# Four score banks in one tile, token preparation in three steps, and cosine norms taken apart in a four-layer transformer kernel

## The chip, the cores and the metric

The kernel runs on one core of a Trainium2 chip, in one launch. The metric is the device time of that launch in microseconds (us), the median over several runs. The core has a matrix engine (TensorE, PE in the profile, with its weight loads shown apart as PEld), VectorE (DVE), ScalarE (ACT), GpSimd (POOL) and SyncE (SP), from whose queue this kernel issues all of its DMA transfers. Matrix products land in PSUM, which this program uses as eight banks of 128 x 512 fp32. All arithmetic is fp32.

## The reference, cut to what matters

Input `x` has 8 batches of 256 tokens and 512 features. Four layers follow each other:

```python
# layer 0: RMS norm, 8 query heads of width 64 on one key/value head, rotary, softmax; then a gated MLP
h = ada_rms(x);  q, k, v = rope(h @ Wq.T), rope(h @ Wk.T), h @ Wv.T
x = x + softmax(q @ k.T / 8) @ v @ Wo.T
x = x + (silu(h2 @ Wg.T) * (h2 @ Wu.T)) @ Wd.T

# layer 1: LayerNorm with a condition, 16 heads of width 32, cosine attention; then a GELU MLP
qn = q / max(norm(q), 1e-12) * sm          # per token and head, over 32 numbers
kn = k / max(norm(k), 1e-12)
x = x + (softmax(qn @ kn.T + bias) @ v @ Wproj.T + bproj) * gamma1
x = x + (gelu(h2 @ Wfc1.T + bfc1) @ Wfc2.T + bfc2) * gamma2

# layer 2: 16 query heads of width 32, 4 key/value heads, rotary, a sparse mask
x = x + softmax(where(mask, -inf, q @ k.T / sqrt(32))) @ v @ Wo.T

# layer 3: eight experts 64 -> 256 -> 64 on slices of the features, LayerNorm, silu, projection
x = x + silu(layernorm(experts(x)) * (1 + scale) + shift) @ out_W + out_b
```

## The kernel before, in words

The residual `x` stays in SBUF as 16 tiles of 128 tokens. A batch is two such tiles. The stages run one after another: attention 0, MLP 0, attention 1, MLP 1, attention 2, experts.

**Order.** The program is traced in Python and a planner then orders the instructions of each engine: it may run an instruction earlier than the trace order has it, as soon as its inputs and its buffer are free, and it puts the semaphore waits in. A tile belongs to a tag; a tag has as many buffers as `BUFS` says, and a new tile of a tag waits until the users of the tile before it in its buffer are done.

**PSUM.** Two tags share the eight banks. Tag `C` has four buffers of one bank: projections, transposes, weighted sums. Tag `A` has four buffers of one bank as well: the scores of the four heads of a group (`scored`, L645), the four accumulators of the MLP's second product (`lower`, L955), and the hidden values of the experts (L1621).

**Attention** (`attend`). The loop runs over batches `b` and groups `g` of four heads: two groups in a batch in layer 0, four in layers 1 and 2. One turn traces the scores of this group (`scored`), transposes of two heads of the group before (`turned`, L702, with copies out of PSUM on L460 and L464), the softmax of this group (`softmax`: L667 or L659 on DVE, exponentials L672 on ACT, reciprocals of the sums sent through DRAM by the SP queue, L685 and L690), then slices of queued work (`some`: the projection of the next batch, the output product of the batch before), the other two transposes, the weighted sum (`weighted`, L717) and its division (`divided`, L732). The probability tiles, tag `p`, have seven buffers.

**Preparation** (`prepare`, `normed`, `fetch`, `h`). Two batches ahead, after the softmax of group 0, the tokens of a batch are normalised for their projection: statistics (L431, L432), the power -1/2 on POOL (L440), the two normalisations (L450), a DVE transposition in 32 x 32 blocks (L515), four DMAs to DRAM (L520). `fetch` brings them back, feature-major, in eight DMAs (L539), or in one for an MLP (L533). `h` scales and shifts them (L472, L474). The target tag `hT` has two buffers.

**Cosine norms** (`project1`, layer 1). For each of the two token tiles of a batch, the product of the queries goes to SBUF with its bias (L1367) and is squared (L1369) and summed by heads (L1370); the keys are copied (L1373), squared out of SBUF (L1375) and summed (L1376). POOL then takes the maximum with 1e-24 (L1378) and the power -1/2 (L1379) of all 32 sums in one instruction each, multiplies the query half by `sm` (L1380), and multiplies queries and keys by their norms (L1383). Their transposes are L1355.

**MLP** (`mlp`). Both products use a Strassen scheme of seven products. `lower` accumulates in four banks over four steps `p`; after the fourth, `combined` reads them (L966 on ACT, L968 to L973 on DVE), and the next `lower` with `p == 0` takes four banks anew.

Of the kernel before, what the change touches and what calls it, by code (L numbers as in the profile page):

```python
# [28 lines left out]
AF = mybir.ActivationFunctionType  # L29
ALU = mybir.AluOpType  # L30
# [3 lines left out]
P = 128  # L34
# [5 lines left out]

BUFS = {
    "n": 4, "hT": 2, "qT": 2, "kT": 2, "v": 2, "ctxT": 6, "p": 7, "qk": 4, "row": 3, "wbig": 8,
    "A": 4, "C": 4,
}
MASKED = -1.0e30

# [125 lines left out]
class Program:  # L172
# [21 lines left out]

    def bank(self, tag):
        return self.t([P, 512], tag)

# [219 lines left out]

    def normed(self, xs, eps, rms=False, outs=None):


        nc = self.nc
        n = len(xs)
        mv = self.t([P, n, 2], f"mv{n}", 2)
        r = self.t([P, n], f"r{n}", 2)
        for i, x in enumerate(xs):
            st = self.t([P, 6], "st", 3)  # L430
            nc.vector.bn_stats(st, x)  # L431
            nc.vector.bn_aggr(mv[:, i, :], st)  # L432
        mean, var = mv[:, :, 0], mv[:, :, 1]
        if rms:
            nc.vector.tensor_tensor(r, mean, mean, ALU.mult)
            nc.vector.tensor_tensor(r, r, var, ALU.add)
            nc.gpsimd.tensor_scalar(r, r, eps, None, ALU.add)
        else:
            nc.gpsimd.tensor_scalar(r, var, eps, None, ALU.add)  # L439
        nc.gpsimd.tensor_tensor(r, r, self.neg_half[:, 0:n], ALU.pow)  # L440
        rows = []
        for i, x in enumerate(xs):
            if outs is None:
                y = self.bank("n")
            else:
                y, x = outs[i], x.rearrange("p (k c i) -> p c k i", k=KC, c=4)
            if rms:
                nc.vector.tensor_scalar(y, x, r[:, i : i + 1], None, ALU.mult)
            else:
                nc.vector.tensor_scalar(  # L450
                    y, x, mv[:, i, 0:1], r[:, i : i + 1], ALU.subtract, ALU.mult
                )
            rows.append(y)
        return rows
# [47 lines left out]
    def prepare(self, name, b, quick=False):  # L502

        eps, _, _, _, rms, blocks = self.stage(name)
        xs = [self.x[TB * b + t] for t in range(TB)]
        hT = self.t([P, KC * S], "hT")
        if quick:
            self.ready[name, b] = [hT, self.normed(xs, eps, rms), None, 0]  # L510
            return
        nc = self.nc
        y = hT.rearrange("p (c k t i) -> p c k t i", c=4, k=KC, t=TB)
        self.normed(xs, eps, rms, [y[:, :, :, t, :] for t in range(TB)])
        nc.vector.transpose(hT, hT)  # L515
        kept = self.turns[self.n_turn % 3]
        self.n_turn += 1
        to = kept.rearrange("(c i) (a x) -> a i c x", c=4, a=4)
        for a in range(4):
            nc.sync.dma_start(  # L520
                to[a], hT[32 * a : 32 * a + 32, :].rearrange("p (c x) -> p c x", c=4)
            )
        self.ready[name, b] = [hT, None, kept, 0]

    def fetch(self, calls):

# [14 lines left out]
    def h(self, name, b, quick=False):  # L541


        if (name, b) not in self.ready:
            self.prepare(name, b, quick)
            yield None
            self.fetch(1)
        hT, rows, _, at = self.ready[name, b]
        while self.calls < at:
            yield None  # L550
        self.ready.pop((name, b))
        _, mod, scale_at, shift_at, _, blocks = self.stage(name)
        if blocks:
            place = hT.rearrange("p (a k q) -> p k a q", a=4, k=KC)
        else:
            place = hT.rearrange("p (k t) -> p k t", k=KC)

        def placed(i, c, in_):
            scale = mod[:, scale_at + c, b : b + 1]
            shift = None if shift_at is None else mod[:, shift_at + c, b : b + 1]  # L560
            self.modulated(i, place[:, c], in_, scale, shift)

        if rows is None:
            for c in range(KC):
                placed(c, c, place[:, c])
        else:

            def evacuate(c0, m):
                for c in range(2):
                    placed(c0 // 2, c0 + c, m[:, c, :])  # L570

            yield from self.feature_major(rows, evacuate)
        if blocks:
            return hT
        hT = place
        return hT
# [32 lines left out]
    def attend(self, name, n_groups, hd, project, value, finish, work, key_tiles=(2, 2), biased=None,  # L609
# [26 lines left out]

        def scored(b, g):
            lhs_rhs = [got[b][0](g, j) for j in range(4)]
            s = [self.bank("A") for _ in range(4)]
            rows = P // hd  # L640
            for j0 in range(0, 4, rows):
                for q in range(TB):
                    for j in range(j0, j0 + rows):
                        lhsT, rhs = lhs_rhs[j]
                        nc.tensor.matmul(  # L645
                            s[j][:, at[q] : at[q] + wide[q]], lhsT(q), rhs(wide[q]),
                            start=True, stop=True,
                        )
            return s
# [86 lines left out]
            chunks = ctx.pop(b)  # L736
            return finish(b, lambda k, t: chunks[k][:, t * P : (t + 1) * P])

        last = None
        for i in range(B * n_groups + 1):  # L740
            ahead = None
            if i < B * n_groups:
# [18 lines left out]
            if ahead is not None:  # L761
                ahead = (b, g, softmax(ahead[2]))
                if g == 0 and ahead_of:
                    for c in (1, 2) if b == 0 else (b + 2,):
                        if c < B:
                            self.prepare(name, c, quick=c == 1)
                        elif c == B and after is not None:
                            self.prepare(after, 0)
                elif g == 0 and b == B - 1:
                    self.prepare(after, 0)  # L770
            if last is None:
                self.some(3 * quantum)
            elif ahead is None and then is not None:
# [118 lines left out]
    def mlp(self, ups, downs, down_sums, load_ups, load_down, act, h, finish, tail):  # L892
# [52 lines left out]
        def lower(s, a, sums_of_a):  # L945
            hh, b, p = where(s)
            (y11, t3, y21, y22), (t1, t2, t4) = downs[4 * hh + p][:2]
            if p == 0:
                acc[:] = [self.bank("A") for _ in range(4)]
            s1, s2, s4 = [sums_of_a[:, i, :] for i in range(3)]  # L950
            for at, half, left, right in (
                (0, 0, a[:, 0, :], y11), (0, 1, a[:, 2, :], y21), (3, 0, a[:, 1, :], t3),
                (2, 0, s1, t1), (2, 1, s2, t2), (1, 0, s4, y22), (1, 1, a[:, 3, :], t4),
            ):
                nc.tensor.matmul(  # L955
                    acc[at][:, half * S : (half + 1) * S], left, right,
                    start=(p == 0 and half == 0), stop=(p == 3), skip_group_check=True,
                )
            if p == 3:
                combined(hh, b)  # L960
# [373 lines left out]
    def project1(self, b, got):  # L1334
# [8 lines left out]
        def part(t, i):  # L1343
            m = self.bank("C")
            yield from self.product_steps(
                m,
                lambda k: hT[:, k, t * P : (t + 1) * P],
                lambda k: w[:, k, i * D : (i + 1) * D],
            )
            return m  # L1350
# [11 lines left out]
        ready = []  # L1362
        for t in range(TB):
            ss = self.t([P, 32], "ss", 2)
            q = yield from part(t, 0)
            qs = self.bank("qk")
            nc.vector.tensor_tensor(qs, q, self.q_bias, ALU.add)  # L1367
            sq = self.bank("n")
            nc.scalar.activation(sq, qs, AF.Square)  # L1369
            nc.vector.tensor_reduce(ss[:, 0:16], heads(sq), AX.X, ALU.add)  # L1370
            k_ = yield from part(t, 1)
            ks = self.bank("qk")
            nc.scalar.copy(ks, k_)  # L1373
            sq = self.bank("n")
            nc.scalar.activation(sq, ks, AF.Square)  # L1375
            nc.vector.tensor_reduce(ss[:, 16:32], heads(sq), AX.X, ALU.add)  # L1376

            nc.gpsimd.tensor_scalar(ss, ss, 1e-24, None, ALU.max)  # L1378
            nc.gpsimd.tensor_tensor(ss, ss, self.neg_half, ALU.pow)  # L1379
            nc.gpsimd.tensor_tensor(ss[:, 0:16], ss[:, 0:16], self.sm, ALU.mult)  # L1380
            for y, at in ((qs, 0), (ks, 16)):
                by = ss[:, at : at + 16].unsqueeze(2).to_broadcast([P, 16, 32])
                nc.gpsimd.tensor_tensor(heads(y), heads(y), by, ALU.mult)  # L1383
            ready.append((qs, ks))
        qT = self.t([P, KC, S], "qT")
        kT = self.t([P, KC, S], "kT")
        v = self.t([P, TB, D], "v")
# [216 lines left out]
    def layer3(self):  # L1604
        nc = self.nc
        n_tiles = 4
        b1, b2 = self.v("b1"), self.v("b2")

        def two(tag):
# [4 lines left out]
        def hidden(xT, k):  # L1614

            got = [[], []]
            for f in range(2):
                ms = [self.bank("A") for _ in range(2)]
                for j in range(2):
                    rows = slice(64 * j, 64 * j + 64)  # L1620
                    nc.tensor.matmul(  # L1621
# [130 lines left out]
```

## Time and profile before

| | us |
|---|---|
| median of three runs | 2130.87 (2130.27 to 2134.04) |
| the profiled execution's own time | 2125.73 |
| its span | 2123.8 |
| PE busy in it | 2060.5 (97%) |
| DVE busy | 1349.5 (64%) |
| ACT busy | 761.1 (36%) |
| POOL busy | 291.3 (14%) |

The profile is of one execution. Its span is the time from the first to the last instruction; busy time is the time in which an engine executes. "PE C L702 <- DVE p L460" says that PE waited, before an instruction of line 702 that writes a tile of tag `C`, for DVE's instruction of line 460 that wrote a `p`. An fp32 product appears as two records. Stages by the trace: attention 0 until about 304 us, MLP 0 until about 905, attention 1 until about 1296, MLP 1 until about 1700, attention 2 until about 1968, experts until the end.

### The profile page before, as it was taken

The page shows a single profiled execution, that of the slowest core. Times are in us where ns is not written, and L with a number is a line of the kernel's source. Part 1 is how long each engine was busy: PE and PEld are TensorE (multiplying, and loading weights), DVE is VectorE, ACT ScalarE, POOL GpSimd, SP SyncE. Part 2 cuts the span into 40 slices and gives each one's busy share as a digit, 9 for nine tenths or more (in the row PEclk, how much of TensorE's full clock was granted, in tenths as well). Part 3 has the DMA queues.
Part 4 walks back from the last instruction along what each step waited for, and adds up shares of the span by engine and source line. Part 5 has one row for each costly group of instructions (what it writes and reads, how often), then busy time and mean ns, then how long its engine had stood idle before and what let it go on. Part 6 is the DMA issues. An engine that isn't in the chain of part 4 may idle for free.

```text
span 2123.8 us, 36492 instructions
## 1 busy us (share of the span) xinstructions
PE 2060.5 (97%) x13282; PEld 1523.8 (72%) x13282; DVE 1349.5 (64%) x4474; ACT 761.1 (36%) x2330; POOL 291.3 (14%) x308
## 2 busy tenths in 40 slices
PE   7999899999999999999999999999999989999999
PEld 4555569999999999855555547999999855555444
DVE  6856665656676555756666665776666777776333
ACT  3424321111111111245555663222222256566644
POOL 1101100000000000144444432000000101010220
PEclk9999999999999999999999999999999999999999
DMA  8320241211230100411112132233211222210001
GB/s 308 115 59 17 91 149 38 73 41 58 76 94 19 36 19 18 100 46 40 37 40 52 44 95 78 85 102 115 94 49 46 76 47 45 57 39 19 11 35 40
DMA packets 172147, 138.18 MB, mean 65 GB/s; under 512 B 77824, under 2 KB 144064, under 8 KB 171968
## 3 DMA queue, kind: packets, MB, share of 16 engines
q1 hardware_dynamic: 171968, 135.86, 21.6%
q8 instruction: 105, 1.72, 0.3%
q14 instruction: 74, 0.61, 0.1%
HBM read 99.87 MB, written 35.95 MB: 64 GB/s over the span
## 4 chain that ended last, share of the span: by engine, by line
PE 81%; DVE 8%; DMA 5%; ACT 2%; POOL 2%; issue 1%; SPq 1%; DVEq 0%; ACTq 0%; POOLq 0%
PE C L908 28%; PE C L585 20%; PE A L955 18%; PE C L702 4%; PE A L645 4%; PE C L717 3%; DMA wqkv<-spread 2%; DVE p L667 1%; PE A L1621 1%; DMA spread<-invT 1%; ACT p L672 1%; PE C L1639 1%; DMA turn<-hT 1%; DMA hT<-turn 1%; DVE p L460 1%
## 5 line engine op out<-in xcount | busy, mean ns | idle before, releaser
L908 PE MATMUL C<-hT,wbig 128*128 128x128 f32 x3072 | 416.3, 275 | 0.0
L908 PEld LDWEIGHTS C<-hT,wbig 128*128 128x128 f32 x3072 | 388.8, 192 | 8.6 <-issue 1.8
L585 PE MATMUL C<-wqkv,hT 128*128 128x512 f32 (+1 forms) x768 | 311.1, 545 | 4.9 <-DVE p L460 3.9
L908 PE MATMUL C<-ctxT,wbig 128*128 128x128 f32 x2160 | 300.0, 275 | 0.0
L672 ACT ACTIVATE p<-p,low 128x256 f32<-128x256 f32 (+1 forms) x512 | 241.9, 475 | 152.7 <-DVE low L667 152.0
L908 PEld LDWEIGHTS C<-ctxT,wbig 128*128 128x128 f32 x2160 | 270.1, 192 | 0.0
L955 PE MATMUL A<-wbig,p 128*128 128x256 f32 x1024 | 242.5, 379 | 0.0
L585 PEld LDWEIGHTS C<-wqkv,hT 128*128 128x128 f32 x768 | 130.9, 191 | 124.7 <-issue 111.2
L667 DVE CUSTOM_DVE_ANT_0 p<-A,row 128x256 f32<-128x256 f32 (+1 forms) x512 | 171.7, 386 | 70.6 <-PE C L717 55.1
L955 PEld LDWEIGHTS A<-wbig,p 128*128 128x128 f32 x1024 | 189.6, 190 | 23.0
L702 PEld LDWEIGHTS C<-ident,p 128*128 128x128 f32 x1152 | 129.3, 142 | 81.3 <-issue 39.6
L925 ACT COPY p<-C 128x128 f32<-128x128 f32 x192 | 51.3, 267 | 371.6 <-PE C L908 370.9
L936 DVE TENSOR_TENSOR p<-p,C 128x256 f32<-128x256 f32 x192 | 79.3, 421 | 162.7 <-PE C L908 160.8
L702 PE MATMUL C<-ident,p 128*128 128x128 f32 x1152 | 165.2, 282 | 15.2 <-DVE p L460 6.8
L585 PE MATMUL C<-wo,ctxT 128*128 128x512 f32 x336 | 158.7, 604 | 5.6 <-DVE ctxT L732 5.5
L439 POOL TENSOR_SCALAR r<-mv 128x2 f32<-128x2 f32 (+1 forms) x28 | 7.2, 256 | 953.0 <-DVE mv L432 953.0
L1276 ACT ACTIVATE p<-C 128x128 f32<-128x128 f32 x64 | 17.8, 278 | 295.9 <-DVE p L936 295.9
L926 DVE TENSOR_TENSOR p<-p,C 128x128 f32<-128x128 f32 x192 | 54.9, 286 | 101.5 <-ACT p L925 99.4
L460 DVE COPY p<-C 128x512 f32<-128x512 f32 (+1 forms) x160 | 100.7, 630 | 23.8 <-PE C L702 23.4
L585 PEld LDWEIGHTS C<-wo,ctxT 128*128 128x128 f32 x336 | 58.7, 190 | 70.5 <-issue 53.8
L672 ACT ACTIVATE p<-A,low 128x256 f32<-128x256 f32 x128 | 59.3, 478 | 120.5 <-DVE low L659 87.9
L464 ACT COPY p<-C 128x512 f32<-128x512 f32 (+1 forms) x160 | 85.5, 535 | 36.0 <-PE C L702 36.0
(226 smaller groups left out, 3064.7 us busy)
## 6 DMA issues: line engine op xcount, KB each, us to landing
turn<-hT SPq DMA_DIRECT2D x120, 128.0 KB
hT<-turn SPq DMA_DIRECT2D x16, 512.0 KB
kept<-hT SPq DMA_DIRECT2D x16, 512.0 KB
hT<-kept SPq DMA_DIRECT2D x16, 512.0 KB
wbig<-spread SPq DMA_DIRECT2D x64, 128.0 KB
hT<-turn SPq DMA_DIRECT2D x112, 64.0 KB
wbig<-in_wada1T SPq DMA_DIRECT2D x6, 1024.0 KB
ctxT<-kept SPq DMA_DIRECT2D x48, 128.0 KB
```

What stands on the lines that cost most here:

```text
L460: self.nc.vector.tensor_copy(out, in_)
L464: self.nc.scalar.copy(out, in_)
L585: self.nc.tensor.matmul(out, lhsT(k), rhs(k), start=(k == 0), stop=(k == n - 1))
L645: nc.tensor.matmul(s[j][:, at[q] : at[q] + wide[q]], lhsT(q), rhs(wide[q]), start=True, stop=True,)
L667: nc.vector.tensor_tensor_reduce(p[:, cols], s[j][:, cols], biased[:, cols], -1.0, BIG, ALU.add, ALU.min, low[:, q : q + 1],)
L672: nc.scalar.activation(p[:, cols], src[:, cols], AF.Exp, bias=low[:, q : q + 1], scale=sign, accum_out=tot[:, j, q : q + 1],)
L702: nc.tensor.transpose(m[:, n * P : (n + 1) * P], p[:, at[q] + k * P : at[q] + (k + 1) * P], self.ident,)
L717: nc.tensor.matmul(o[i * hd : (i + 1) * hd, c * S + q0 * P : (c + 1) * S], value(got[b][1], g, j, k), pT[j][:, mine[0] * P : (mine[-1] + 1 ...
L908: nc.tensor.matmul(m[:, c : c + P], w[:, k * P : (k + 1) * P], b[:, k], start=(first and k == 0), stop=(k == steps - 1), skip_group_check= ...
L926: nc.vector.tensor_tensor(g[:, 0, :], g[:, 0, :], m[:, P : 2 * P], ALU.add)
L936: nc.vector.tensor_tensor(g[:, 1:3, :], g[:, 0, :].unsqueeze(1).to_broadcast([P, 2, P]), m[:, 2 * P : 4 * P].rearrange("p (i t) -> p i t", ...
L955: nc.tensor.matmul(acc[at][:, half * S : (half + 1) * S], left, right, start=(p == 0 and half == 0), stop=(p == 3), skip_group_check=True,)
```

## The change

1. Tag `A` becomes one buffer of four banks. `four` takes it and hands out its banks. `scored` and `lower` use it; the experts take it once and alternate between its halves.
2. `normed` and `prepare` become generators. In attention 1 and 2, from batch 1 on, the preparation is traced in three pieces behind the softmax of groups 0, 1 and 2: statistics and power; first normalisation; second normalisation, transposition and the DMAs to DRAM. The fetch follows in the turn in which the last piece is traced.
3. In `project1`, maximum, power and multiplications are traced for the queries and for the keys apart, 16 columns at a time, each after its own sums; the keys are squared from PSUM, and then copied.

```diff
-    "A": 4, "C": 4,
+    "A": 1, "C": 4,
...
+    def four(self):
+        t = self.t([P, 4, 512], "A")
+        return [t[:, i, :] for i in range(4)]
...
-    def normed(self, xs, eps, rms=False, outs=None):
+    def norms(self, xs, eps, rms=False, outs=None):
...
         nc.gpsimd.tensor_tensor(r, r, self.neg_half[:, 0:n], ALU.pow)
         rows = []
         for i, x in enumerate(xs):
+            yield
...
         hT = self.t([P, KC * S], "hT")
+        self.ready[name, b] = [hT, None, None, math.inf]
...
-        self.normed(xs, eps, rms, [y[:, :, :, t, :] for t in range(TB)])
+        yield from self.norms(xs, eps, rms, [y[:, :, :, t, :] for t in range(TB)])
         nc.vector.transpose(hT, hT)
...
-        self.ready[name, b] = [hT, None, kept, 0]
+        self.ready[name, b][2] = kept
...
-            s = [self.bank("A") for _ in range(4)]
+            s = self.four()
...
-                            self.prepare(name, c, quick=c == 1)
+                            steps.append(self.prepare(name, c, quick=c == 1))
                         elif c == B and after is not None:
-                            self.prepare(after, 0)
+                            steps.append(self.prepare(after, 0))
                 elif g == 0 and b == B - 1:
-                    self.prepare(after, 0)
+                    steps.append(self.prepare(after, 0))
+
+                for step in steps:
+                    for _ in step:
+                        if b > 0 and ahead_of:
+                            break
+                    else:
+                        done.append(step)
+                steps[:] = [step for step in steps if step not in done]
...
-                acc[:] = [self.bank("A") for _ in range(4)]
+                acc[:] = self.four()
...
+            both = []
+            for i in range(2):
+                m = yield from part(t, i)
+                y = self.bank("qk")
+                sq = self.bank("n")
+                if i == 0:
+                    nc.vector.tensor_tensor(y, m, self.q_bias, ALU.add)
+                    nc.scalar.activation(sq, y, AF.Square)
+                else:
+                    nc.scalar.activation(sq, m, AF.Square)
+                    nc.scalar.copy(y, m)
+                r = ss[:, 16 * i : 16 * i + 16]
+                nc.vector.tensor_reduce(r, heads(sq), AX.X, ALU.add)
+
+                nc.gpsimd.tensor_scalar(r, r, 1e-24, None, ALU.max)
+                nc.gpsimd.tensor_tensor(r, r, self.neg_half[:, 0:16], ALU.pow)
+                if i == 0:
+                    nc.gpsimd.tensor_tensor(r, r, self.sm, ALU.mult)
+                by = r.unsqueeze(2).to_broadcast([P, 16, 32])
                 nc.gpsimd.tensor_tensor(heads(y), heads(y), by, ALU.mult)
+                both.append(y)
+            ready.append(both)
...
+        banks = self.four()
...
-                ms = [self.bank("A") for _ in range(2)]
+                ms = [banks[(2 * k + f) % 2 * 2 + j] for j in range(2)]
```

More of the change, by code (lines that the diff above doesn't have):

```diff
@@ L418, in ada_23, with normed @@
         yield 2.3
-    def normed(self, xs, eps, rms=False, outs=None):
+    def normed(self, *args):
+        steps = self.norms(*args)
+        while True:
+            try:
+                next(steps)
+            except StopIteration as e:
+                return e.value
+    def norms(self, xs, eps, rms=False, outs=None):
         nc = self.nc
@@ L508, in prepare @@
         hT = self.t([P, KC * S], "hT")
+        self.ready[name, b] = [hT, None, None, math.inf]
         if quick:
-            self.ready[name, b] = [hT, self.normed(xs, eps, rms), None, 0]
+            self.ready[name, b][3] = 0
+            self.ready[name, b][1] = self.normed(xs, eps, rms)
             return
@@ L544, in h @@
         if (name, b) not in self.ready:
-            self.prepare(name, b, quick)
+            for _ in self.prepare(name, b, quick):
+                pass
             yield None
@@ L737, in outcome @@
             return finish(b, lambda k, t: chunks[k][:, t * P : (t + 1) * P])
-        last = None
+        last, steps, done = None, [], []
         for i in range(B * n_groups + 1):
@@ L1364, in project1 @@
             ss = self.t([P, 32], "ss", 2)
[L1365 to L1382, printed above, removed]
+            both = []
[16 more added lines that the diff above has]
+                by = r.unsqueeze(2).to_broadcast([P, 16, 32])
                 nc.gpsimd.tensor_tensor(heads(y), heads(y), by, ALU.mult)
-            ready.append((qs, ks))
+                both.append(y)
+            ready.append(both)
         qT = self.t([P, KC, S], "qT")
```

## The prediction

> **What bounds the kernel now.** First the page: the busy line of PE, and the chain.
>
> ```profile
> PE 2060.5 (97%) x13282; PEld 1523.8 (72%) x13282; DVE 1349.5 (64%) x4474; ACT 761.1 (36%) x2330; POOL 291.3 (14%) x308
> PE 81%; DVE 8%; DMA 5%; ACT 2%; POOL 2%; issue 1%; SPq 1%; DVEq 0%; ACTq 0%; POOLq 0%
> ```
>
> PE is idle for 2123.8 - 2060.5 = 63.3 us in all. Then the windows by stage: length, then PE busy.
>
> ```profile
> 100.00:304.00 204.00, 191.32 (x1066) 115.07 (x1067) 128.63 (x355) 71.80 (x245) 26.04 (x44) 0.98 0.23 68
> 304.00:905.00 601.00, 601.00 (x4461) 569.19 (x4460) 377.35 (x1216) 96.78 (x291) 14.88 (x21) 1.00 0.18 56
> 905.00:1296.00 391.00, 378.50 (x2197) 204.37 (x2196) 246.31 (x846) 217.35 (x669) 164.63 (x121) 0.99 0.20 52
> 1700.00:1968.00 268.00, 253.93 (x1789) 145.38 (x1789) 196.75 (x879) 161.03 (x609) 29.25 (x38) 0.99 0.18 41
> ```
>
> The MLPs have no idle PE; attention 1 has 12.5 us and attention 2 14.1. The change adds no work to PE, so it can win only there and in PE time that is busy for a bad reason. The timeline of PE in one batch of attention 2 shows such time:
>
> ```profile
> 1780.06 0.94 PE L645 MATMUL A<-kT,qT 32*128 32x128 f32 x16
> ...
> 1784.17 0.48 PE L645 MATMUL A<-kT,qT 32*128 32x128 f32 x2
> ...
> 1789.20 0.93 PE L645 MATMUL A<-kT,qT 32*128 32x128 f32 x14
> ...
> 1796.49 1.70 PE L645 MATMUL A<-kT,qT 32*128 32x128 f32 x16
> 1798.13 0.87 PE L702 MATMUL C<-ident,p 128*128 128x128 f32 x6
> ```
>
> One group of scores is 16 records: four heads, each on its own 32 rows of the array. Together they take 0.94 us. In the second group of the batch the planner ran the first head (x2) alone, as soon as its bank was free; the other three came 5 us later, and took as long as four. The last group takes 1.70 us, because it goes at the pace at which DVE frees its banks. The timeline of DVE shows whose bank:
>
> ```profile
> 1796.58 0.29 DVE L667 CUSTOM_DVE_ANT_0 p<-A,row 128x128 f32<-128x128 f32 x1 [1.16 <-PE C L717]
> ```
>
> This is the fourth head of the group before: it had to wait for the weighted sum (L717), which gives back the `p` buffer it writes. So bank four is read out only after that sum, with the next scores already begun.
>
> **The four banks, part by part.** *Split groups.* Attention 2 has six split 2 + 14. Less the overlap with their neighbours the pieces occupy PE for 0.41 and 0.86 us, a whole group 0.87: 0.40 us each, 6 x 0.40 = 2.4 us. One tile can't be taken bank by bank, so this goes whole.
>
> *Slow groups.* Seven are of the 1.70 us kind: 0.76 us over 0.94. In one tile the first score waits for the fourth head's read. If the planner puts the transposes that follow (0.87 us, of the group before, their exponentials done) into that wait, 7 x 0.76 = 5.3 us is won; if not, the wait is the same, and as much as the first two records' 0.48 us is lost, -3.4. I take half the gain, 2.7.
>
> A rule of the Trainium skill speaks against all this ("Perfetto Trace Analysis", Optimization Strategy): the same gap recurring on the engine that should be saturated can mean that PSUM is short for the next tile. By that rule one buffer instead of four spreads the 0.76 us to all 32 groups of this stage, 24 us lost instead of the 5.1 won that I take. The rows decide for me: in attention 1 a regular group is ready 1.0 to 3 us after the last read, with a projection's product (1.98 us) between.
>
> *Layer 0.* Scores occupy PE for 39.2 us there; sixteen groups at the commonest 1.93 would be 30.9. The 8.3 us more lie in the first 80 us and around 140, where heads go singly. Between 0 and 8.3 I take 2.0: this start waits on the exponentials anyway.
>
> *MLPs.* A whole tile makes the first `lower` product of a block wait for L973, the last reader. From the timelines of DVE and PE at such a seam:
>
> ```profile
> 1325.95 0.42 DVE L973 TENSOR_TENSOR n<-n,A 128x256 f32<-128x256 f32 x1
> ...
> 1327.56 1.68 PE L955 MATMUL A<-wbig,p 128*128 128x256 f32 x7
> ```
>
> L973 ends at 1326.37 and the weight load of L955 starts at 1327.45: 1.1 us to spare, at every seam of MLP 1 but one (-0.3); MLP 0 has 3.6 us or more. Cover: six to fourteen products of L908. Cost 0.5 us; if DVE ran 1 us later at each of 15 seams it would be some 15 us at most.
>
> *Seams into attention.* Scores of attention 2 start at 1700.04 while L973 ends at 1701.65; a whole group would end 0.2 us later than now. The second group waits there anyway, 3.6 us for L667, and a pause costs clock: granted 0.91 from 1700 to 1738, 1.00 afterwards. I add 0.5 for all seams (0 to 4).
>
> **Preparation in three steps.** A batch is 2 x 0.69 (L431) + 0.2 (L432) + 2 x 0.55 (L450) + 1.24 (L515) = 3.9 us of DVE, two POOL operations, four DMAs out and eight back on SP. Nothing is removed. The trace shows that it is not run where it is traced: the statistics at 1776.9 belong to the tokens normalised at 1806.5, a batch later, and in attention 1 L450 runs at 1060.40, before the scores behind whose softmax it stands. So the steps change priorities, not positions, unless DVE has no free moment. What they could win is the time for which PE waits for copies behind that work: all of "PE C L702 <- DVE p L460" is 6.8 us, of which attention 2 has 2.0. What they could lose: hT of the batch is ready at 1791.05 and used at 1807.77, 16.7 us to spare; two groups later is 17.0, so 0.3 us in each of the five batches made in steps there (1 to 5), 1.5. From a gain of 4 to a loss of 2 I take 0, the cover being DVE's 36% idle time. The SP queue is the first rival.
>
> **Cosine norms.** POOL's power of 32 columns is 5.45 us (L1379), of 2 columns 0.715 (L440): 0.158 us per column, so 16 columns are 0.715 + 14 x 0.158 = 2.9 us. The keys' chain behind their sums falls from 0.29 + 5.45 + 0.22 + 2 x 1.05 = 8.1 us to 0.3 + 2.9 + 1.05 = 4.3, if POOL is free, and starts 0.6 us earlier without the copy ahead; the queries no longer wait for the keys' sums. POOL's sum rises by some 16 x 0.7 us, in an engine busy 14%. All this was hidden but for one wait:
>
> ```profile
> PE C L1355 <- POOL qk L1383: 1.2, 1, 1.2
> ```
>
> That is won: 1.2 us. Against it, the keys' bank of `C` is held by a square (0.63 us) more, 16 times, 10 us at most; I take 0, since among all waits none of PE's names the copy that frees that bank today (L1373).
>
> **Sum.** Won: 2.4 + 2.7 + 2.0 + 1.2 = 8.3. Lost: 0.5 + 0.5, and 1.0 for copies that now stand behind eight score reads in a row (0.35 us each) instead of two and six. Net -6.6 us on a profiled execution of 2125.73 (span 2123.8). That one ran 5.1 us under the median; the difference carries over: 2130.9 - 6.6 = 2124.3. About 0.2%, 4.3 us, is what a measurement of this kernel can tell from no change.
>
> **Rivals.** *The transfers back land in front of the softmax sums: slower.* SP issues in order, in attention 2:
>
> ```profile
> 1782.88 5.79 SPq L539 DMA_DIRECT2D hT<-turn  x8
> 1790.23 0.56 SPq L685 DMA_DIRECT2D spread<-invT  x1
> 1792.19 0.54 SPq L690 DMA_DIRECT2D wbig<-spread  x1
> ```
>
> Today the eight fall between two groups. Traced two groups later they can stand ahead of L685 or L690, whose rows the division (L732) needs some 5 us later; it has about 2.5 us to spare (issued by 1792.7, needed near 1797). 5.8 - 2.5 = 3.3 us in five batches is 16.5 us, and DVE's later reads of scores queue behind L732. With the -6.6 that is +10: 2141. It decides from the point at which the eight are issued less than 3 us before an L690. In attention 1, with 12 us per group, they are covered. For it: SP's row is that dense; against: order is the planner's, which hoisted them so far. A chance of 0.20.
>
> *Single waits become whole ones: slower.* If no work fills the waits, the slow groups cost 3.4, the seams 4 and the lost head start of one head 0.7 each in six groups, 4: some 11, less the certain 2.4 + 1.2, +8: 2139. Chance 0.12.
>
> *Nothing to measure.* The three steps are already made by the planner and PE's savings come back as other waits, as behind L1138 and L702 in attention 2, 0.5 us each per batch: 2129 to 2133. Chance 0.16.
>
> *More.* All of the slow groups (5.3), half of layer 0's excess (4.2) and the two waits of 0.46 and 0.59 us at copies in each of seven batches of attention 1 (7.4) go as well: 2.4 + 5.3 + 4.2 + 1.2 + 7.4 = 20.5: 2110. Chance 0.14. The forecast itself, 2117 to 2126.5, keeps 0.38.
>
> **How the numbers follow.** Faster: 0.38 + 0.14 = 0.52. Same 0.16, slower 0.32. Both signs have much of it: the likeliest case alone would be 2117 to 2126.5. The range runs from just beyond *more* to just beyond the first rival: 2108 to 2143.
>
> **What would show it.** Right: every group of L645 in attention 2 as x16 within 0.95 us, none as x2 and x14; PE busy in the MLPs unchanged; L1379 in 32 instructions near 2.9 us; no wait of L1355 on POOL; L450 still far from its softmax. Wrong: L645 waiting for L667 more than the 3.6 us of now; PE waiting for L973; L732 waiting for the rows from `spread` (now 14.7 and 6.1 us); a lower granted clock at a batch's start; PE waiting for hT.

## The result, and the profile after

The changed kernel takes 2152.43 us (median of four runs, 2151.77 to 2154.14), the kernel before 2130.57 beside it. The ratio is 1.0104, 95% interval [1.0086, 1.0121]. It is slower by about 22 us, well beyond the 4.3 us that a measurement of this kernel can tell, and outside the predicted range of 2108 to 2143. The profiled execution took 2154.14 us, span 2152.2.

The page first: the busy line and the chain.

```profile
PE 2072.5 (96%) x13282; PEld 1513.1 (70%) x13282; DVE 1346.4 (63%) x4474; ACT 755.5 (35%) x2326; POOL 303.0 (14%) x340
PE 83%; DMA 6%; DVE 5%; ACT 3%; SPq 2%; issue 1%; POOL 1%; DVEq 0%; ACTq 0%; POOLq 0%
```

The span grew by 28.4 us. Of these PE is *busy* 2072.5 - 2060.5 = 12.0 us more, with the same 13282 records, and idle 16.4 us more. Where that lies, the stages tell. Below, a stage begins with its first product (scores L645, MLP L908, experts L1621, and their lines after), so the borders are not the rough ones given with the profile before; the length is in us:

| stage | before | after | difference | PE busy | PE idle |
|---|---|---|---|---|---|
| attention 0 | 263.5 | 266.1 | +2.5 | -2.9 | +5.4 |
| MLP 0 | 626.7 | 630.1 | +3.5 | +0.2 | +3.3 |
| attention 1 | 368.6 | 359.1 | -9.6 | -2.7 | -6.9 |
| MLP 1 | 413.4 | 419.5 | +6.1 | +0.6 | +5.5 |
| attention 2 | 268.4 | 271.8 | +3.3 | -4.1 | +7.5 |
| experts | 155.4 | 177.7 | +22.3 | +21.1 | +1.2 |

The windows of the changed kernel over attention 1, attention 2 and the experts (length, then PE busy; the clock stands before the last two columns):

```profile
924.00:1283.00 359.00, 354.39 (x2102) 188.62 (x2102) 237.24 (x826) 209.38 (x662) 164.07 (x142) 0.98 0.20 50
...
1703.00:1974.00 271.00, 249.44 (x1788) 138.30 (x1789) 194.48 (x871) 159.90 (x609) 29.36 (x38) 0.97 0.17 40
1974.00:2152.00 178.00, 172.74 (x601) 66.48 (x599) 54.45 (x104) 74.73 (x124) 23.21 (x23) 1.00 0.07 25
```

Two things stand out. Attention 1 became *shorter*; and most of the loss is in the experts, a stage that the prediction did not cost, and there it is busy time of PE at full clock (1.00 in the last window).

**The experts.** The groups of PE in that stage, the two products on either side of the GELU, before (L1621, L1639) and after (L1649, L1667):

```profile
L1621 PE MATMUL A<-qk,wbig 64*128 64x512 f32 x128 | 34.0, 618 | 0.0
L1639 PE MATMUL C<-p,wbig 128*64 128x512 f32 x128 | 29.9, 601 | 0.0
```

```profile
L1667 PE MATMUL C<-p,wbig 128*64 128x512 f32 x128 | 47.3, 613 | 1.6 <-ACT p L1656 1.6
L1649 PE MATMUL A<-qk,wbig 64*128 64x512 f32 x128 | 40.6, 641 | 0.0
```

The mean of one record hardly moves (600 to 641 ns), but the time that 128 of them occupy rises by 6.6 and 17.4 us: they lie beside each other less. The timelines of PE and ACT show how. Before:

```profile
1986.27 4.82 PE L1621 MATMUL A<-qk,wbig 64*128 64x512 f32 x16
1991.02 1.94 PE L1639 MATMUL C<-p,wbig 128*64 128x512 f32 x8
...
1987.49 4.16 ACT L1628 ACTIVATE p<-A,vec 128x512 f32<-128x512 f32 x7 [3.01 <-PE A L1621]
```

After:

```profile
1987.55 1.13 PE L1649 MATMUL A<-qk,wbig 64*128 64x512 f32 x4
1988.61 1.93 PE L1667 MATMUL C<-p,wbig 128*64 128x512 f32 x4
1990.47 1.13 PE L1649 MATMUL A<-qk,wbig 64*128 64x512 f32 x4
...
1988.73 1.26 ACT L1656 ACTIVATE p<-A,vec 128x512 f32<-128x512 f32 x2 [1.65 <-PE A L1649]
1991.71 1.26 ACT L1656 ACTIVATE p<-A,vec 128x512 f32<-128x512 f32 x2 [1.72 <-PE A L1649]
```

Before, sixteen records run through and the GELUs run beside them. After, a pair of products (x4), then two GELUs, then the next pair: PE fills the turn shown with the products behind earlier GELUs, one column half of the array at a time (the code gives each expert of a pair 64 of the columns). Their x4 takes 1.93 us, as long as an x8 before. In the records, before, the two halves start 0.01 us apart (1991.02 and 1991.03); after, in this turn, each record starts 0.38 to 0.48 us behind the last. A turn is 1990.47 - 1987.55 = 2.92 us; before, the same work takes (4.82 + 3.65) / 4 = 2.1 us (L1639 has a run of sixteen in 3.65). Not every turn is like this one: in some, whole-array products fill the wait. Over the stage the two products together occupy PE for 85.5 us instead of 63.4: some 22 us more, which is the stage's loss.

**The MLPs.** At the seam that the prediction read, before, PE's step and ACT's first copy:

```profile
1321.41 3.19 PE L955 MATMUL A<-wbig,p 128*128 128x256 f32 x14
1323.03 0.57 ACT L966 COPY qk<-A 128x512 f32<-128x512 f32 x1
```

and after:

```profile
1318.03 3.19 PE L980 MATMUL A<-wbig,p 128*128 128x256 f32 x14
1321.31 0.58 ACT L991 COPY qk<-A 128x512 f32<-128x512 f32 x1 [1.57 <-PE A L980]
```

The copy of the first accumulator started 1.6 us before the step's end (1324.60); now it starts after it (1321.22). The 1.1 us by which L973 was ahead of the next block is used up: the next L980's weight load starts 0.12 to 0.22 us after the last reader (L998, which was L973) at every seam of MLP 1, and PE stalls at two. PE's waits of the whole kernel after:

```profile
PE A L662 <- DVE n L998: 6.3, 2, 3.2
...
PE A L980 <- DVE n L998: 2.3, 2, 1.2
```

The first line is the two seams from an MLP into an attention, 3.1 and 3.2 us:

```profile
1702.76 1.66 PE L662 MATMUL A<-kT,qT 32*128 32x128 f32 x16 [3.20 <-DVE n L998]
```

### The profile page after: what moved, and what is told of

It reads as the page before. It is cut to its first block, busy times and chain, and to the rows that moved or that the text cites. A ratio compares the mean times of both kernels' runs of the same rounds, so it can differ in the third digit from the quotient of the medians.

```text
span 2152.2 us, 36493 instructions
## 1 busy us (share of the span) xinstructions
PE 2072.5 (96%) x13282; PEld 1513.1 (70%) x13282; DVE 1346.4 (63%) x4474; ACT 755.5 (35%) x2326; POOL 303.0 (14%) x340
## 4 chain that ended last, share of the span: by engine, by line
PE 83%; DMA 6%; DVE 5%; ACT 3%; SPq 2%; issue 1%; POOL 1%; DVEq 0%; ACTq 0%; POOLq 0%
PE C L933 27%; PE C L602 20%; PE A L980 17%; PE C L719 4%; PE C L734 4%; PE A L662 3%; PE C L1667 2%; PE A L1649 2%; ACT p L689 2%; DMA hT<-turn 2%; DMA wqkv<-spread 1%; DVE p L684 1%; SPq L555 1%; DMA spread<-invT 1%; PE C L1163 1%
## 5 line engine op out<-in xcount | busy, mean ns | idle before, releaser
L980 PE MATMUL A<-wbig,p 128*128 128x256 f32 x1024 | 243.8, 379 | 2.3 <-DVE n L998 2.3
L980 PEld LDWEIGHTS A<-wbig,p 128*128 128x128 f32 x1024 | 189.0, 190 | 25.3 <-issue 2.7
L719 PEld LDWEIGHTS C<-ident,p 128*128 128x128 f32 x1152 | 130.5, 143 | 77.1 <-issue 44.2
```

What stands on the lines that cost most here:

```text
L719: nc.tensor.transpose(m[:, n * P : (n + 1) * P], p[:, at[q] + k * P : at[q] + (k + 1) * P], self.ident,)
L980: nc.tensor.matmul(acc[at][:, half * S : (half + 1) * S], left, right, start=(p == 0 and half == 0), stop=(p == 3), skip_group_check=True,)
```

## The experiments

Each kernel is the one before, or the changed one, with one thing different, timed against the kernel before. Stage lengths are of the profiled execution, cut as above.

**Only the tile taken back.** The changed kernel with four one-bank tiles behind the same function:

```diff
-    "A": 1, "C": 4,
+    "A": 4, "C": 4,
...
-        t = self.t([P, 4, 512], "A")
-        return [t[:, i, :] for i in range(4)]
+        return [self.bank("A") for _ in range(4)]
```

> The changed kernel, but the four banks are four tiles of one bank each (the experts still take theirs once); the three steps and the separate norms stay. Theory T (a tile is followed as a whole: a reader of one bank waits for the last write to any of the four, a writer for all readers): the experts' stage goes back from 177.7 to about 155 us, the seams into attention from 3.1 us of idle PE to under 1.5, attention 1 stays near 359; about 2121 us, some 31 under the changed kernel. Rival R1 (the experts lose because their banks are taken once instead of anew for each pair, which changes the order): the experts stay at 177, about 2143 us. Rival R2 (the loss comes from the steps or the norms): about 2152 us.

Measured: 2126.55 us, ratio 1.0009 [1.0001, 1.0018]; experts 155.4, MLP 1 413.8, attention 1 370.4. The loss goes with the tile, and so does the gain in attention 1, which had been expected to stay. The experts still take their banks once and alternate between halves, so that part of the edit is not the cause; that the four banks are one tile is.

**Only the tile.** The kernel before with one tile of four banks in the attentions, the MLPs and the experts, and no other part of the change:

```diff
-            s = [self.bank("A") for _ in range(4)]
+            s = self.four()
...
-                acc[:] = [self.bank("A") for _ in range(4)]
+                acc[:] = self.four()
...
+        banks = self.four()
...
-                ms = [self.bank("A") for _ in range(2)]
+                ms = [banks[(2 * k + f) % 2 * 2 + j] for j in range(2)]
```

> The kernel before with the one tile of four banks alone (scores, MLP accumulators, experts). Theory T: experts near 177, seams 3 us each, copies of the first accumulator after the end of the whole step; attention 1 near 369, since its gain is from the norms or the steps: about 2158 us. If the one tile also gives attention 1 its 9.6 us, by keeping scores together: about 2150 us. Rival R2 (steps or norms to blame): 2124 to 2131 us.

Measured: 2153.34 us, ratio 1.0131 [1.0117, 1.0145]; experts 177.7, attention 1 358.0, MLP 1 418.8. The tile alone makes the whole loss, and the gain in attention 1 as well.

**Only the cosine norms.** The kernel before with part 3 of the change alone.

> The kernel before with the separate cosine norms and the keys squared from PSUM alone. If the 9.6 us that attention 1 gained in the changed kernel are theirs: attention 1 near 360, about 2122 us. My prediction's step: 1.2 us won, 2129 us. Rival (the gain is of the steps or the one tile): 2129 to 2132 us.

Measured: 2127.95 us, ratio 1.0017 [1.0008, 1.0026]; attention 1 370.8. POOL's power, before and then in this kernel:

```profile
L1379 POOL TENSOR_TENSOR ss<-ss,neg_half 128x32 f32<-128x32 f32 x16 | 87.2, 5453 | 1.3
```

```profile
L1380 POOL TENSOR_TENSOR ss<-ss,neg_half 128x16 f32<-128x16 f32 x31 | 90.6, 2924 | 2.6
```

The instruction costs what was worked out, 2.92 us. (31 of its 32 instructions lie in the window of this view.) But the wait of the transposes on POOL's product is still there, 1.1 us instead of 1.2.

**Only the preparation in steps.** The kernel before with part 2 alone.

> The kernel before with the preparation in three steps alone. My prediction's step: 0, that is 2130 us, with the normalisation near the same times as now. If the gain of attention 1 is theirs: about 2122 us. If the transfers back now stand in front of the softmax sums in attention 2: attention 2 near 285 instead of 268, about 2145 us.

Measured: 2126.08 us, ratio 1.0002 [0.9993, 1.0012]. No stage moves by more than 1.1 us.

The other eight kernels are the kernel before with the `A` banks of each stage in a pool of its own, so that the size of the tile can be chosen stage by stage; none has the steps or the norms apart. The pools themselves change little: with the experts' table below, the five other stages are within 1.5 us of before.

```diff
+A_TILE = {"attention0": 1, "mlp0": 1, "attention1": 4, "mlp1": 1, "attention2": 1, "experts": 1}
...
+    def banks(self, n):
+        per = min(self.a_per, n)
+        out = []
+        for _ in range(n // per):
+            t = self.t([P, per, 512], "A", 4 // per)
+            out += [t[:, i, :] for i in range(per)]
+        return out
...
-            s = [self.bank("A") for _ in range(4)]
+            s = self.banks(4)
```

**One tile in attention 1 alone** (the table as shown).

> The kernel before, with one tile of four banks for the scores of attention 1 alone (layers 1 and 2's joint attention stage in the middle); attentions 0 and 2, the MLPs and the experts keep four one-bank tiles, as before. Theory T (a tile of four banks is followed as one thing: a reader of any bank waits for the last write to the tile, a writer for the last reader; what that costs depends on the order of the copies around it): attention 1 falls from 368.6 to about 359 us as in the changed kernel, because VectorE's copies of finished transposes come after two score reads instead of five; the seam before it costs 0 to 3 (the scores still wait for the MLP's last copy). Whole kernel 7 to 11 us below the before, ratio near 0.996. Rival (the gain in attention 1 comes from what the other stages with one tile do to it, as work moved over the seam): attention 1 stays at 367 to 370 and the whole kernel is within 2 us of the before.

Measured: 2116.57 us, ratio 0.9941 [0.9928, 0.9953]; attention 1 357.7. The gain is that stage's own.

**One tile in all attentions** (`"attention0": 4, "attention1": 4, "attention2": 4`).

> The kernel before, with one tile of four banks for the scores in all three attentions; the MLPs and the experts keep one-bank tiles. Theory T: attention 1 falls by about 10 us, attention 0 lengthens by 2.5 and attention 2 by 1 to 3.3 (the splits go and the idle time comes back), the MLPs and the experts as before: whole kernel 2 to 8 us below the before. Rival (the experts or the MLPs lose because the attentions hand their banks over as one tile): 10 to 25 us above it.

Measured: 2121.95 us, ratio 0.9967 [0.9954, 0.9979]; attention 0 266.4, attention 1 356.7, attention 2 269.8, experts 155.4. As expected, attentions 0 and 2 give some of it back: 2.8 and 1.4 us of the 11.9 that attention 1 wins. Some 4 us more go at the seams, in the lengths of the MLPs before them (628.8 and 415.1).

**The experts in two tiles of two banks** (`"experts": 2`, the other stages 1).

> The kernel before, with the experts' banks as two tiles of two banks each, every pair of banks in one tile; all else in one-bank tiles. Theory T: the products of one pair can again run while ScalarE reads the other pair; only a GELU of one bank of a pair waits for the pair's other products. Experts 155 to 160 us, whole kernel within 5 us of the before. Rival (any tile of more than one bank makes this stage alternate, as four banks in one tile did): experts 170 to 178 us and the whole kernel 15 to 23 above the before.

Measured: 2127.97 us, ratio 0.9991 [0.9982, 1.0]; experts 156.1. A tile of a pair costs 0.7 us there, a tile of two pairs 22.3. What cost was that one pair's GELU and the other pair's products exclude each other.

**One tile in the MLPs alone** (`"mlp0": 4, "mlp1": 4`, the other stages 1).

> The kernel before, with one tile of four banks in the two MLPs alone. Theory T: the copy of the first accumulator starts after the step's last product instead of 1.0 us before it, so 2 to 3 us are lost in MLP 1, and at each of the two seams into an attention up to 3 us, since the scores wait for the MLP's last copy: whole kernel 3 to 10 us above the before, MLP 1 at 415.5 to 420 us instead of 413.4. Rival (the seams' 3 us belong to the attentions' own tile): MLP 1 at 413 to 416 and the whole kernel within 3 us of the before.

Measured: 2131.14 us, ratio 1.0009 [0.9999, 1.002]; MLP 1 419.6, MLP 0 630.0, attention 1 364.7, attention 2 268.3. The lengths of the MLPs are those of the changed kernel, so their own tile is enough for their loss, seams included. A tile in the attentions alone makes part of the seams too: with attention 1's alone MLP 0 takes 628.6 us, with that of all three MLP 1 takes 415.1. Against medians the whole kernel loses 1.8 us, less than was expected; the profiled execution has a span 7.8 us above that of before (2131.6 and 2123.8), so the size of this loss stays open. Some comes back behind the seam of 3.06 us, where the first block of attention 1 (the first of its eight batches) is 1.98 us shorter (45.22 instead of 47.20). That the other engines have run ahead in the pause is a reading of this, not shown.

What makes attention 1 faster? The order of DVE's instructions, which run one after another. Before, around one group (PE, then DVE; L702 are transposes, L667 reads of scores, L460 the copy of finished transposes):

```profile
1041.54 1.09 PE L702 MATMUL C<-ident,p 128*128 128x128 f32 x8
...
1045.24 0.63 PE L702 MATMUL C<-ident,p 128*128 128x128 f32 x4 [0.46 <-DVE p L460]
...
1044.07 0.42 DVE L667 CUSTOM_DVE_ANT_0 p<-A,row 128x256 f32<-128x256 f32 x1
1044.41 0.69 DVE L460 COPY p<-C 128x512 f32<-128x512 f32 x1
```

The eight transposes end at 1042.6. DVE then does five of the group's eight score reads (1042.69 to 1044.4) before it copies them out, and PE stands 0.46 us for the bank. With one tile the group can't be read before its last head is written, and the planner puts the copy (L479) after two reads (L687). With the tile in attention 1 alone, DVE and then PE:

```profile
1039.52 0.42 DVE L687 CUSTOM_DVE_ANT_0 p<-A,row 128x256 f32<-128x256 f32 x1
1039.87 0.69 DVE L479 COPY p<-C 128x512 f32<-128x512 f32 x1
...
1040.68 1.04 PE L722 MATMUL C<-ident,p 128*128 128x128 f32 x8
```

If it is the order, the same can be had without the tile.

**The transposes traced first.** One-bank tiles throughout; in attention 1 the two `turned` of the group before stand ahead of this group's `scored`:

```diff
+                if name == "attention1" and last is not None:
+                    for j in range(2):
+                        turned(j, last[2][0][j])
                 ahead = (b, g, scored(b, g))
-            if last is not None:
+            if last is not None and (name != "attention1" or ahead is None):
                 for j in range(2):
                     turned(j, last[2][0][j])
```

> The kernel before, all in one-bank tiles; in attention 1 the transposes of two heads of the group before are traced ahead of this group's scores instead of behind them, so that VectorE copies the first of them out of PSUM before this group's score reads instead of after five of the eight. Theory C (the one tile pays in attention 1 because it puts that copy earlier, after two score reads; the tile itself brings nothing): attention 1 falls from 368.6 to 357 to 363 us, whole kernel 5 to 12 us below the before. Rival (it pays because scores then run and are read as whole groups): attention 1 stays at 366 to 371 and the whole kernel within 2 us of the before.

Measured: 2118.14 us, ratio 0.9951 [0.9936, 0.9967]; attention 1 354.8. The copy (now L479) stands ahead of all reads, and the transposes (L722) behind it run whole:

```profile
1038.85 1.04 PE L722 MATMUL C<-ident,p 128*128 128x128 f32 x8
...
1035.86 0.68 DVE L479 COPY p<-C 128x512 f32<-128x512 f32 x1
```

Theory C holds: the order alone brings what the tile brought. Blocks three to six of the stage, where the clock is 1.00 in every profile, take 183.8 us with this order, 183.5 with the one tile and 190.9 before. That the whole stage is shorter than the expected 357 is luck: its first block ran at full clock (last section). The edit moves the transposes together with their copy; which of the two counts was not tried.

**Attentions 0 and 2 in two tiles of two banks** (`"attention0": 2, "attention1": 4, "attention2": 2`).

> The kernel before, with the scores of attention 1 in one tile of four banks and those of attentions 0 and 2 in two tiles of two banks; MLPs and experts in one-bank tiles. Theory T (what a tile of several banks costs is the wait for its other banks, so half as much with two): attention 0 within 2 us and attention 2 0 to 2 us longer than before, attention 1 about 357 us, whole kernel 8 to 13 us below the before, about level with one tile in attention 1 alone. Rival (attentions 0 and 2 lose by any tile of more than one bank): attention 0 2.5 and attention 2 1.5 to 3 us longer, whole kernel only 5 to 8 below the before.

Measured: 2135.00 us, ratio 1.0023 [1.0013, 1.0033]; attention 0 275.6, attention 1 356.8, attention 2 274.3. Half the tile costs more than the whole one: +12.1 and +5.9 us. Theory T is wrong there as a measure of size, and the rival's numbers are too small as well. In attention 0 one place, told below, is about 6 of the 12.1 us; for attention 2 no cause was sought.

**Attention 1 in two tiles of two banks** (`"attention1": 2`).

> The kernel before, with the scores of attention 1 in two tiles of two banks each; all else in one-bank tiles. Theory C (what pays in attention 1 is when VectorE copies the transposes): the gain follows the place of the copy among the eight score reads, and as two banks are written anew before the other two are read it should come late again: attention 1 at 363 to 369 us, whole kernel 0 to 5 us below the before. Rival (whole tiles pay in themselves): attention 1 at 357 to 361, whole kernel 8 to 13 below.

Measured: 2121.38 us, ratio 0.9963 [0.9949, 0.9977]; attention 1 363.0. The stage is at the edge of what theory C gave; the whole kernel, 7.2 us below the before, lies between the two ranges. In the order of DVE the copy comes after four reads. Put beside each other, the steady blocks (three to six) of attention 1 follow the place of that copy: after five reads 47.4 to 48.3 us (before), after four 46.7 to 46.8, after two 45.87 (one tile), ahead of all 45.96 (transposes first). From two reads to none nothing more is won.

**Transposes first in attentions 1 and 2**, one-bank tiles throughout.

> The kernel before, all in one-bank tiles; in attentions 1 and 2 the transposes of two heads of the group before are traced ahead of this group's scores. Theory C (a copy that VectorE makes behind score reads holds the transposes up): attention 1 about 355 us as with that order there alone, and attention 2, whose blocks also idle 0.55 us before a transpose, 1 to 4 us shorter than the 268.4 of before; whole kernel 12 to 17 us below the before. Rival (in attention 2 the copies behind the score reads cost nothing that PE's order does not give back): attention 2 at 267.5 to 272, whole kernel 7 to 13 below.

Measured: 2116.83 us, ratio 0.9945 [0.9924, 0.9965]; attention 1 360.1, attention 2 266.9. The stage as a whole hardly gains (its other one-bank versions lie between 267.3 and 268.8), and the whole kernel, 9.9 us below the before, is in the rival's range. But its first block ran at a granted clock of 0.83, against 0.82 to 0.91 in the others, and took 39.16 us, the longest of them; blocks two to seven take 195.8 us against 197.9 to 199.7, a gain of 2 to 4 us as theory C has it. So neither is settled there. This kernel, the one with one tile in attention 1 and the one with the transposes first in attention 1 beat the kernel before by some 0.5%; the runs do not rank the three.

## Why the prediction was wrong, point by point

*The step that failed* is the one under "The four banks, part by part" that asks what a tile of four banks makes wait. It followed only the writer: the next score, or the next `lower` product, waits for the last reader. The reader was left out: the first read of *any* bank now waits for the last write to the tile. Two terms were wrong for that reason, and a third stage, the experts, had none: a 0 without a reason where 22.3 us were lost. The prediction's own sign of being wrong, PE waiting for L973, is what the profile shows: 6.3 + 2.3 us.

- *Experts: no term in the sum.* Measured 22.3 us, as much as the whole kernel lost in the end. The rows were in the profile: "PE L1621 x16" with seven GELUs beside it is a stage in which a reader works inside the writer's run. With one tile both sides bind there: the GELUs start behind their pair's last product (1988.73 after 1988.68), and the next pair's products behind the GELUs (1990.47 after 1989.99).
- *MLPs, predicted 0.5.* Measured 2.3 us of stalls in MLP 1. The text gave the danger itself ("if DVE ran 1 us later at each of 15 seams") but named no reason for it. There was one: the first copy lost its start of 1.6 us, the whole chain of readers moved with it, and the 1.1 us to spare fell to 0.12 to 0.22.
- *Seams into attention, predicted 0.5 for all.* Measured stalls of 3.1 and 3.2 us. The step took L973 at its old time; DVE's first read came 0.78 us after the end of the last product instead of 0.73 us ahead of it (1700.34 against 1699.56; 1699.38 against 1700.11), and the group of scores ended 2.35 us later, counted from that end, not 0.2. In the MLP experiment some 2 us of a seam came back in the first block.
- *Split and slow groups, 5.1 won.* They went as foretold: of 32 groups in attention 2, 29 are one x16 of 0.94 us (the others are the first two, at the seam, and one of 1.24), and PE is busy with scores for 32.5 us instead of 44.2. In all it is busy for 4.1 us less. But more than that came back as idle time (+7.5 us). The timeline of PE, last scores of a batch and its last weighted sum:

```profile
1800.11 0.94 PE L662 MATMUL A<-kT,qT 32*128 32x128 f32 x16
...
1804.60 0.84 PE L734 MATMUL C<-p,kT 128*32 128x256 f32 x10 [0.58 <-ACT p L478]
```

  The last scores stand 25.8 us behind the batch's first (1774.27); before, they stood 24.3 behind (1796.49 and 1772.24). Their reads, exponentials and copies come as much later, and the weighted sums wait for those copies, 0.20 and 0.58 us in each of five batches (4.4 us in all with one more). This is read from the traces; no run took these waits away. The half gain of 2.7 us, "if the planner puts the transposes into that wait", looked at PE's filling and not at who is late next.
- *Layer 0, 2.0 won.* Measured +2.5. DVE's order again: a sum of MLP weights, traced elsewhere, now stands in front of the copy that PE's transposes wait for, and waits for its own transfer. DVE:

```profile
139.43 0.43 DVE L839 TENSOR_TENSOR wbig<-wbig 128x256 f32<-128x256 f32 x1 [4.89 <-DMA wbig<-in_wuT]
```

  and PE:

```profile
142.80 1.11 PE L497 MATMUL C<-ident,n 128*128 128x128 f32 x4 [6.14 <-DVE p L474]
```

  In the kernel with two banks to a tile the same happens (DVE waits 6.02 us for such a transfer, PE 5.99 us for DVE). All three kernels with one tile in attention 0 have this wait of PE there (5.8 to 6.1 us), and none with one-bank tiles has one of 2 us or more around that place (125 to 155 us). That it is the cause is still read from the traces; no run took it away, and kernels with one-bank tiles already spread over 261.2 to 265.5 us in this stage.
- *Preparation in steps, 0.* Right: 1.0002. The rival of transfers ahead of the softmax sums fell with it: DVE's division waits for those rows 24.0 us in all, 23.0 before.
- *Cosine norms, 1.2 won.* The instruction's price was right (2.9 worked out, 2.92 measured), the gain was not: the wait is 1.1 us instead of 1.2, and alone the edit is 0.17% slower, under the 0.2% bound. Some 1 to 2 us of that lie in attention 1: 370.8, and 370.4 in the changed kernel with one-bank tiles, against 368.6 to 369.6 without the edit (where the MLPs have one-bank tiles too). PE waits there for DVE's copies ahead of the projection (L585) for 5.1 us instead of 2.9. Why those copies come later was not tried.
- *The rival "single waits become whole ones", 2139,* had half of the mechanism at a chance of 0.12: whole waits, but the writer's alone, and priced in the attentions and at the seams alone. Its 4 for the seams is the nearest to the 6.3 measured. *"More"* foresaw that the 0.46 and 0.59 us waits at copies in attention 1 could go: they did, and that stage's 9.6 us are larger than the 7.4 given.
- *The rule of the Trainium skill* that was weighed ("Perfetto Trace Analysis", Optimization Strategy) had the direction right, as a warning that PSUM is short for the next tile, and was set aside on rows of attention 1 alone. Its sign, a recurring gap on the saturated engine, is not what the largest loss looks like here: PE's idle time in the experts rose by 1.2 us only, its busy time by 21.1. The 24 us worked out by it for attention 2 were not lost there (3.3).
- *The sum* has a slip: 8.3 won less 2.0 lost is 6.3, not 6.6; it changes nothing in the account.

The sum of the parts as measured: -9.6 in attention 1, +2.5 and +3.3 in the other attentions, +9.6 in the MLPs with their seams, +22.3 in the experts, and 0.2 ahead of them: +28.3 of the span's 28.4. Against medians it is 22 us: the profiled execution of before ran 4.8 us under the 2130.57, that of the changed kernel 1.7 over its median.

## What to carry to other kernels

A tile of several banks binds both sides: ask not only who must wait to write it, but which read now runs inside the writer's run, and do so in every stage that takes the tile. A loss need not show as idle time: compare the time that a given number of records occupies. And where one engine both reads new work and frees the bank of finished work, the order of its instructions can be worth more than the buffers: tracing the transposes ahead of the scores gave 0.5% with no other change.

## What the runs showed of the hardware

Products on 64 of the array's columns cost half as much when both halves start together: eight records in 1.94 us (L1639), against four in 1.93 us when they start one after the other (L1667). In the changed kernel itself four L1667 that start in pairs take 1.08 us (2011.03). And a block can take 11% longer by the granted clock alone. The first block of attention 1 took 43.12 us with the transposes first there, and 47.95 us, in the same order of instructions on every engine, with the transposes first in attention 2 too. In the second the granted clock was 0.50 from 926 to 936 us; PE's idle time in the block is 1 us in both. The windows of the first and then of the second kernel (the clock stands before the last two columns):

```profile
918.00:961.00 43.00, 42.00 (x244) 23.28 (x244) 31.06 (x110) 25.86 (x82) 16.98 (x12) 1.00 0.14 48
```

```profile
920.00:968.00 48.00, 47.00 (x244) 25.48 (x248) 31.51 (x111) 26.08 (x82) 16.97 (x12) 0.89 0.13 43
```

So a few us in the first block of an attention say nothing of a kernel. In attention 1 the granted clock of that block lies between 0.85 and 1.00 over the fourteen profiles; blocks two to seven, at 1.00 in all of them, are the ones to compare.
